# A deformable convolution after a recurrence: constants and borders placed before the recurrence, table rows written in 1 KB runs, the offsets' products ordered ahead of the turning

## The chip, the cores and the metric

The kernel runs on one core of one Trainium2 chip. The metric is the device time of one execution in microseconds, lower is better. Everything is float32, and one launch computes four layers of a network.

## The reference, cut to what matters

The input x has 4 images of 128 channels and 64 x 64 pixels. Each of four layers adds a convolution-like block and then a token block to x. The change lies where the token block of layer 0 (a recurrence) meets the convolution of layer 1 (a deformable one):

```
# layer 0, token block: tokens of an image in order, yt of 128 channels
Wx = batchnorm(layernorm(t) @ W.T)
yt = sigmoid(Wx[t] + yt @ V.T)            # one step after another
x  = x + y

# layer 1, deformable convolution, 3 x 3 taps
z    = layernorm over channels (x)
off  = conv3x3(z, w_off) + b_off          # 18 channels: dy, dx for each of 9 taps
mask = sigmoid(conv3x3(z, w_mod) + b_mod) # 9 channels
for each pixel and tap k:
    (py, px) = pixel + tap + (dy, dx)
    v = bilinear(z at the four pixels around (py, px), zero outside the image) * mask
x = x + sum over k of weight[:, :, k] @ v[k] + bias
```

## The kernel before, in words

x stays in SBUF as `net.xs`, channels on the 128 partitions, 4 x 4096 pixels along them. The phases follow one another in `PHASES`: `involution`, `recurrence`, `deformable`, then `expert_choice` and others. Inside a phase, `manual_schedule` fixes the order of PE, ACT, DVE and POOL to the order in which the Python code emits instructions; every engine works through its list in order. SP, which issues the ordinary transfers, also has one list in order. Transfers take turns over eight semaphores, so a transfer can wait for the one eight places before it. Where a pool's memory was used by an earlier phase, the first writer waits for that phase's last reader.

**Recurrence** (`recurrence`, lines 452 to 587). SP loads `rnn_w`, `rnn_wt`, `rnn_vt` and two vectors (L473 to L480). PE's first instruction is a product of `rnn_vt` with itself (L514); behind it come the layer norm (L181 and so on), the statistics, and two sweeps of the recurrence (L564, L569). The last sweep adds its states to `net.xs` (L575). POOL only clears two small tiles (L485).

**Deformable convolution** (`deformable`, lines 590 to 908). For each image a *table* in DRAM holds, for each of 66 x 66 positions, the 128 channels of the four pixels around it: 2 KB, so that one gathered row serves one bilinear sample. The code first loads the weights (`dcn_wk`, `dcn_woff`, `dcn_boff`, `dcn_bias`), clears `dcn_zero`, makes two grids of coordinates (L638, L640), and clears two padded images (`padded_pair`, L247). `plan(b)` then prepares one image:

- borders of the table are written from `dcn_zero` (L667, L669), 16 transfers per image;
- the layer norm into the padded image: centred products (L686), copies (L689), squares (L694), variances (L676), the root and reciprocal (L700, L704), and scaling (L710, L715);
- turning: for each of four groups of 16 rows, PE turns pixels onto 64 partitions (L724), ACT copies them to one of two `dcn_xt` buffers (L726), and SP writes that buffer four times to the table (L731), once for each of the four neighbours, 512 bytes per run;
- the offsets' products: 2 x 36 products over the padded image (L744), bias (L753), turning (L757), copies (L762);
- `places`: index and the four bilinear weights (L772 to L806), with the mask's sigmoid on ACT (L793).

For image 0 all of `plan(0)` comes first. Then, for each image, 288 gathers run on POOL (L816, 128 rows of 2 KB each), two to a step; ACT and DVE weight and add them (L830 to L841), PE turns and adds the two parts (L856, L857), ACT copies (L873), and PE multiplies by the tap's weight (L877). In every step one piece of `plan(b + 1)` is done beside it (`next(side, None)`), so images 1 to 3 are prepared during the gathers of the image before.

Of the kernel before, what the change touches and what calls it, by code (L numbers as in the profile page):

```python
# [17 lines left out]
F32 = mybir.dt.float32  # L18
BF16 = mybir.dt.bfloat16
I32 = mybir.dt.int32  # L20
# [4 lines left out]
PSUM = bass.MemoryType.PSUM  # L25
# [3 lines left out]
P = 128  # L29
B, H, W = 4, 64, 64  # L30
N = H * W
CH = 512
NCH = N // CH
ROWS = CH // W
NT = N // P
# [205 lines left out]
def padded_pair(net, pool, pad, name):  # L241

    side = H + 2 * pad
    out = []
    for i in range(2):
        t = pool.tile([P, side, side], F32, name=f"{name}{i}", bufs=1)
        net.nc.gpsimd.memset(t, 0.0)  # L247
        out.append(t)
    return out
# [202 lines left out]
def recurrence(net):  # L452
# [16 lines left out]
    with ExitStack() as ctx:  # L469
        sb = ctx.enter_context(tc.tile_pool(name="rnn", bufs=1))  # L470
        yp = ctx.enter_context(tc.tile_pool(name="rnn_y", bufs=3))
        w = sb.tile([P, P], F32, name="rnn_w")
# [31 lines left out]
        with (  # L504
# [34 lines left out]
            nc.vector.tensor_sub(shift, gb[:, 1:2], shift)  # L539

        ps = ctx.enter_context(tc.tile_pool(name="rnn_ps", bufs=2, space=PSUM))
        sums = net.xs.rearrange("p b (s t) -> p t b s", t=LEN)
# [46 lines left out]

def deformable(net):  # L590

# [3 lines left out]

    tc, nc, ins = net.tc, net.nc, net.ins
    KK, PAD = 9, 1  # L600
    SIDE = H + 2
    NO = 3 * KK
    Q4 = 4
    BANKS = {"pt": 3, "out": 2, "pd": 1, "pv": 1}
    GATHERED = 14
    with ExitStack() as ctx:
        dram = ctx.enter_context(tc.tile_pool(name="dcn_dram", bufs=1, space=bass.MemoryType.DRAM))
        tables = [dram.tile([SIDE, SIDE, 4, P], F32, name=f"dcn_table{b}") for b in range(B)]
        one = ctx.enter_context(tc.tile_pool(name="dcn", bufs=1))
        sb = ctx.enter_context(tc.tile_pool(name="dcn_s", bufs=2))  # L610
        ps = ctx.enter_context(tc.tile_pool(name="dcn_ps", bufs=2, space=PSUM))
# [4 lines left out]
        nc.sync.dma_start(woff[:, :, 2 * KK : NO], ins["L1_conv_w_mod"])  # L616
        boff = one.tile([P, 1], F32, name="dcn_boff")
        nc.vector.memset(boff, 0.0)
        for q in range(Q4):
            nc.sync.dma_start(boff[32 * q : 32 * q + 2 * KK], ins["L1_conv_b_off"])  # L620
            nc.sync.dma_start(boff[32 * q + 2 * KK : 32 * q + NO], ins["L1_conv_b_mod"])
        wk = one.tile([P, KK, P], F32, name="dcn_wk")
        nc.sync.dma_start(wk, ins["L1_conv_weight"])
        bias = one.tile([P, 1], F32, name="dcn_bias")
        nc.sync.dma_start(bias, ins["L1_conv_bias"])
        zero = one.tile([SIDE, P], F32, name="dcn_zero")
        nc.vector.memset(zero, 0.0)

        grids = []
        for axis in range(2):  # L630
            grid = one.tile([P, NT, KK], I32, name=f"dcn_grid{axis}")
            for half in range(2):
                p = slice(64 * half, 64 * half + 64)
                if axis == 0:
                    pattern, base, step = [[2, NT], [1, 3], [0, 3]], half - 1, 0
                else:
                    pattern, base, step = [[0, NT], [0, 3], [1, 3]], -1, 1
                nc.gpsimd.iota(grid[p], pattern=pattern, base=base, channel_multiplier=step)  # L638
            t = one.tile([P, NT, KK], F32, name=f"dcn_at{axis}")
            nc.vector.tensor_copy(t, grid)  # L640
            grids.append(t)
        pads = padded_pair(net, one, PAD, "dcn_pad")
# [7 lines left out]
        def plan(b):  # L650
# [6 lines left out]
            def bank(tag="pd" if b else "pt"):  # L657
                return ps.tile([P, CH], F32, name=f"dcn_{tag}", tag=tag, bufs=BANKS[tag])

            def inside(c):  # L660
                return xp[:, PAD + c * ROWS : PAD + (c + 1) * ROWS, PAD : PAD + W]


            for q in range(4):
                dy, dx = divmod(q, 2)
                for r in (H, H + 1) if dy else (0, H + 1):
                    nc.sync.dma_start(tables[b][r, :, q, :], zero)  # L667
                for x in (W, W + 1) if dx else (0, W + 1):
                    nc.sync.dma_start(tables[b][1 - dy : 1 - dy + H, x, q, :], zero[0:H])  # L669

# [35 lines left out]
            for c in range(NCH):  # L706
# [9 lines left out]
                yield  # L716
            for c2 in range(NCH // 2):

                xt = sb.tile([W, 2 * ROWS, P], F32, name="dcn_xt", tag="dcn_xt")
                for r0 in range(0, 2 * ROWS, 4):  # L720
                    pt = bank()[0:W].rearrange("p (r c) -> p r c", c=P)
                    for i in range(4):
                        r = PAD + c2 * 2 * ROWS + r0 + i
                        nc.tensor.transpose(pt[:, i, :], xp[:, r, PAD : PAD + W], net.ident)  # L724
                    yield
                    nc.scalar.copy(xt[:, r0 : r0 + 4, :], pt)  # L726
                    yield
                for q in range(4):
                    dy, dx = divmod(q, 2)
                    r0 = 2 * ROWS * c2 + 1 - dy  # L730
                    nc.sync.dma_start(  # L731
                        tables[b][r0 : r0 + 2 * ROWS, 1 - dx : 1 - dx + W, q, :].rearrange("r x c -> x r c"),
                        xt,
                    )

            off = sb.tile([P, NT, NO], F32, name="dcn_off", tag="dcn_off", bufs=1)
            for c4 in range(NCH // Q4):
# [25 lines left out]
                yield  # L763
            yield from places(b, off)

        def places(b, off):
# [32 lines left out]
            nc.vector.tensor_mul(lo, mask, ly)  # L799
            nc.vector.tensor_mul(wq[1], lo, lx)  # L800
            yield
# [3 lines left out]
            nc.vector.tensor_mul(wq[0], lo, lx)  # L805
            nc.vector.tensor_mul(wq[2], hi, lx)  # L806
            made[b] = (tables[b].rearrange("y x q c -> (y x) (q c)"), idx, wq)

        def taken(m, two):
# [876 lines left out]
def top2_experts(net):  # L1686
# [175 lines left out]
    involution,  # L1862
    recurrence,
    deformable,
    lambda net: expert_choice(net, 1),
# [83 lines left out]
```

## Time and profile before

The median of 3 runs is 8233.12 us (8232.96 to 8242.14). The profiled execution took 8237.43 us, of which 8235.6 are the span of its instructions. Busy time of the engines over that span and in three stretches of the stages concerned, in us:

| stretch (us from the span's start) | PE | DVE | ACT | POOL | clock of PE | DMA share |
|---|---|---|---|---|---|---|
| whole span, 8235.6 | 7626.6 | 5525.9 | 3801.2 | 5253.5 | 0.969 | |
| 1030.8 to 1236.7, recurrence | 183.5 | 104.8 | 77.0 | 0.0 | 0.95 | 0.00 |
| 1236.7 to 1331.7, head of the deformable convolution, before the first gather | 51.3 | 32.8 | 18.6 | 11.3 | 0.76 | 0.61 |
| 1331.7 to 2795.7, gathers | 1133.4 | 1247.6 | 638.0 | 1100.7 | 0.94 | 0.77 |

A row of a timeline gives: start in us, length in us, engine, line, operation, out<-in with the shape, and in brackets how long the engine sat idle before it and what released it. A matmul of float32 shows as two entries. PEld is the load of weights, SPq the issuing of transfers on SP. The DMA share is the mean occupied share of the core's 16 DMA engines. A wait for several things is put down to the one that the profile saw come last, which is not always the true one.

### The profile page before, as it was taken

Reading aid. Unit: us, or ns where it says so; the run is one execution under the profiler, and the core shown is the slowest. Engines: PE = TensorE matmul, PEld = TensorE weight load, DVE = VectorE, ACT = ScalarE, POOL = GpSimd, SP = SyncE. Lnnn points to the kernel's source line nnn. Section 1 sums busy time; section 2 is a strip of 40 time slices with the busy share of each in tenths; the row PEclk is TensorE's granted clock in tenths of the full one; section 3 lists DMA queues with packets and bytes.
Section 4 is the critical chain, followed back from the end, with each engine's and each line's share of the span. In section 5 each row is a group of like instructions: output and inputs, shape, how many; then the busy total and the mean of one; then the engine's idle time right before and its main releaser. Section 6 shows DMA issues by size and latency. Waiting matters only on the chain.

```text
span 8235.6 us, 146123 instructions
## 1 busy us (share of the span) xinstructions
PE 7626.6 (93%) x59726; PEld 3315.2 (40%) x59726; DVE 5525.9 (67%) x8715; ACT 3801.2 (46%) x7248; POOL 5253.5 (64%) x2925
## 2 busy tenths in 40 slices
PE   8999986777877889989999999999999999999899
PEld 2222243555555454443444344443444434444333
DVE  7888856888888632237767667766677667677155
ACT  4444433444444430323555555555555555555511
POOL 5989804777777400004888688887888878888700
PEclk9999998999999999988999999999999999999999
DMA  6434206877877430032554445544445445555400
GB/s 182 96 73 96 49 1 164 248 224 234 249 209 209 145 136 0 32 144 47 111 110 100 106 101 108 109 106 103 106 100 111 105 103 107 108 105 109 99 22 23
DMA packets 299127, 944.82 MB, mean 115 GB/s; under 512 B 41876, under 2 KB 114644, under 8 KB 240596
## 3 DMA queue, kind: packets, MB, share of 16 engines
q0 software_dynamic: 142848, 671.18, 34.6%
q1 hardware_dynamic: 155604, 264.26, 11.3%
q8 instruction: 469, 7.68, 0.4%
q14 instruction: 206, 1.69, 0.1%
HBM read 466.78 MB, written 65.88 MB: 65 GB/s over the span
## 4 chain that ended last, share of the span: by engine, by line
PE 57%; DVE 2%; issue 1%; DMA 1%; ACT 1%; POOL 0%; SPq 0%; DVEq 0%; ACTq 0%; POOLq 0%
PE att_pv L1552 15%; PE att_sc L1639 13%; PE att_mx L1496 11%; PE att_sc L1540 5%; PE conv_po L1306 3%; PE top_po L1852 3%; PE top_pw L1828 1%; DVE att_most L1507 1%; DMA moe_w<-in_L_ffn_weight 1%; PE att_sc L1469 0%; PE att_sc L1583 0%; PE top_po L1850 0%; PE att_sc L1600 0%; PE att_mx L1394 0%; PE att_sc L1430 0%
## 5 line engine op out<-in xcount | busy, mean ns | idle before, releaser
L1571 POOL TENSOR_TENSOR att_acc<-att_acc,att_ex 128x2048 f32<-128x2048 f32 x640 | 2902.0, 4534 | 638.5 <-ACT att_ex L1640 619.2
L1507 DVE TENSOR_REDUCE att_most<-att_mx 128x2 f32<-128x1024 f32 x2016 | 2461.8, 1222 | 1070.5 <-PE att_mx L1496 992.6
L1640 ACT ACTIVATE att_ex<-att_sc 128x512 f32<-128x512 f32 x4096 | 2222.9, 595 | 1771.4 <-PE att_sc L1639 1491.4
L1639 PE MATMUL att_sc<-att_q,att_k 32*128 32x512 f32 x8192 | 2455.7, 606 | 0.0
L1496 PE MATMUL att_mx<-att_k,att_q 32*128 32x512 f32 x8064 | 2292.2, 647 | 13.0 <-DVE att_parts L1519 10.8
L1540 PE MATMUL att_sc<-att_rows,att_ones_b 32*128 32x256 bf16 (+1 forms) x6144 | 1502.2, 306 | 4.7 <-ACT att_ex L1640 4.7
L816 POOL DMA_INDIRECT dcn_g<-dcn_table,dcn_idx x1152 | 1100.7, 955 | 436.9 <-DMA dcn_g<-dcn_table,dcn_idx 122.2
L1552 PE MATMUL att_pv<-att_ex,att_vals 128*32 128x256 f32 x16384 | 1309.8, 391 | 0.0
L1496 PEld LDWEIGHTS att_mx<-att_k,att_q 32*128 32x128 f32 x8064 | 610.9, 185 | 867.1 <-issue 707.6
L409 POOL TENSOR_TENSOR inv_prod<-inv_seen,inv_prod 128x512 f32<-128x512 f32 (+1 forms) x672 | 837.5, 1273 | 94.1 <-ACT inv_prod L408 94.1
L411 DVE SCALAR_TENSOR_TENSOR inv_prod<-inv_pk,bspan,inv_seen 128x512 f32<-128x512 f32 (+1 forms) x1120 | 774.6, 743 | 140.2 <-PE inv_pk L398 139.9
L1552 PEld LDWEIGHTS att_pv<-att_ex,att_vals 128*32 128x32 f32 x16384 | 322.5, 108 | 1318.9 <-issue 1300.8
L1639 PEld LDWEIGHTS att_sc<-att_q,att_k 32*128 32x128 f32 x8192 | 818.3, 183 | 10.7 <-issue 8.3
L830 ACT ACTIVATE dcn_one<-dcn_g,dcn_w 128x128 f32<-128x128 f32 x1152 | 457.5, 401 | 790.9 <-DMA dcn_g<-dcn_table,dcn_idx 787.6
L857 PE MATMUL dcn_pt<-ident,dcn_sum 128*128 128x128 f32 x2304 | 516.7, 308 | 242.6 <-DVE dcn_sum L841 241.8
L408 ACT ACTIVATE inv_prod<-inv_pk,bspan 128x512 f32<-128x512 f32 (+1 forms) x672 | 436.1, 682 | 503.8 <-PE inv_pk L398 503.8
L856 PE MATMUL dcn_pt<-ident,dcn_one 128*128 128x128 f32 x2304 | 482.9, 293 | 93.2 <-ACT dcn_st L873 81.1
L856 PEld LDWEIGHTS dcn_pt<-ident,dcn_one 128*128 128x128 f32 x2304 | 397.3, 203 | 305.7 <-issue 137.8
L398 PE MATMUL inv_pk<-inv_red,wtap 32*96 32x512 f32 (+1 forms) x3584 | 511.4, 636 | 7.4 <-DMA inv_seen<-inv_image 7.4
L857 PEld LDWEIGHTS dcn_pt<-ident,dcn_sum 128*128 128x128 f32 x2304 | 371.6, 203 | 322.1 <-DVE dcn_sum L841 321.0
L833 DVE TENSOR_SCALAR dcn_part<-dcn_g,dcn_w 128x128 f32<-128x128 f32 x1152 | 405.8, 352 | 122.5 <-DMA dcn_g<-dcn_table,dcn_idx 89.8
L420 PE MATMUL inv_out<-inv_prod,inv_fold 96*32 96x512 f32 (+1 forms) x3584 | 478.0, 605 | 8.5 <-DVE xs L428 8.5
(339 smaller groups left out, 7090.2 us busy)
## 6 DMA issues: line engine op xcount, KB each, us to landing
att_sum<-att_ex POOLq DMA_DIRECT2D x320, 1024.0 KB, 7.2
inv_seen<-inv_image SPq DMA_DIRECT2D x256, 266.0 KB
moe_w<-in_L_ffn_weight SPq DMA_DIRECT2D x64, 1024.0 KB
dcn_table<-dcn_xt SPq DMA_DIRECT2D x64, 512.0 KB
att_sum<-att_ex SPq DMA_DIRECT2D x32, 1024.0 KB
att_sum<-att_acc POOLq DMA_DIRECT2D x32, 1024.0 KB, 7.2
dcn_g<-dcn_table,dcn_idx POOLq DMA_INDIRECT x1152, 3.7
inv_image<-inv_rows SPq DMA_DIRECT2D x32, 304.0 KB
```

The lines of the kernel that those rows point to most:

```text
L409: nc.gpsimd.tensor_mul(of, view, of)
L411: nc.vector.scalar_tensor_tensor(out=of, in0=as_shape(pk[0:m], of), scalar=by, in1=view, op0=ALU.add, op1=ALU.mult)
L816: nc.gpsimd.indirect_dma_start(out=g, out_offset=None, in_=rows, in_offset=bass.IndirectOffsetOnAxis(ap=idx[:, j + i, k : k + 1], axis=0),)
L856: nc.tensor.matmul(out, one_, net.ident, start=i == 0, stop=False)
L857: nc.tensor.matmul(out, s, net.ident, start=False, stop=i == 3)
L1496: nc.tensor.matmul(pm[i] if alone else pm[:, i, :], q[r, t * P : (t + 1) * P], ks[r, kc * CH : (kc + 1) * CH], start=True, stop=True,)
L1507: nc.vector.tensor_reduce(most[:, 2 * half : 2 * half + 2, kc], pm, AX.X, ALU.max)
L1540: nc.tensor.matmul(pe[:, cols], ones_b[r], lows[g][r, cols], start=cols.start == 0, stop=False)
L1552: nc.tensor.matmul(block["pv"][r, cols], vals[b][:, t, r], ex[:, h, cols], start=t == 0 and half == 0, stop=t == NT - 1 and half == 1,)
L1571: nc.gpsimd.tensor_add(block["acc"], block["acc"], ex)
L1639: nc.tensor.matmul(pe, ks[r, t * P : (t + 1) * P], qs[c][r], start=False, stop=True)
L1640: nc.scalar.activation(ex[:, h, :], pe, AF.Exp)
```

## The change

`PHASES` now holds one phase `recurrence_and_deformable` in the place of two. It opens a pool `dcn_early`, makes a `Sampling` object in it, runs the recurrence, and then the deformable convolution.

- `Sampling` does, ahead of the recurrence in the code, what `deformable` did first: weights, `dcn_zero` (now 512 wide), the grids (one integer tile instead of two; clears and casts on POOL instead of DVE), and the borders of all four tables, now 24 transfers in all instead of 64.
- The table's four neighbours are ordered [dx][dy] instead of [dy][dx], so that two rows of the same column lie side by side. `dcn_xt` gets one more row, copied from the group before; each group is written by two transfers whose runs are two rows of 128 floats, 1 KB, taken from overlapping places of the buffer. After the last group the row below the image is written by two small transfers.
- In `plan` the turning stands behind the offsets' products instead of ahead of them.
- `padded_pair` clears only the four edges of each padded image.
- To make room: `dcn_one` has 14 buffers instead of 15, `dcn_sum` 13 instead of 15, and the pool `rnn_y` is opened only after the recurrence's first part. The weights `wq[1]` and `wq[2]` change places with the table's order.

```diff
@@ padded_pair
-        net.nc.gpsimd.memset(t, 0.0)
+        for edge in (t[:, 0:pad], t[:, pad + H :], t[:, :, 0:pad], t[:, :, pad + W :]):
+            net.nc.gpsimd.memset(edge, 0.0)
@@ recurrence
-        yp = ctx.enter_context(tc.tile_pool(name="rnn_y", bufs=3))
         w = sb.tile([P, P], F32, name="rnn_w")
...
+        yp = ctx.enter_context(tc.tile_pool(name="rnn_y", bufs=3))
         ps = ctx.enter_context(tc.tile_pool(name="rnn_ps", bufs=2, space=PSUM))
@@ 
+class Sampling:
+    def __init__(self, net, one, dram):
+        tc, nc, ins = net.tc, net.nc, net.ins
+        KK = 9
+        SIDE = H + 2
+        self.tables = [dram.tile([SIDE, SIDE, 2, 2, P], F32, name=f"dcn_table{b}") for b in range(B)]
+        zero = one.tile([SIDE, 4 * P], F32, name="dcn_zero")
+        nc.gpsimd.memset(zero, 0.0)
+
+        self.woff = woff = one.tile([P, KK, 32], F32, name="dcn_woff")
+        nc.gpsimd.memset(woff, 0.0)
+        nc.sync.dma_start(woff[:, :, 0 : 2 * KK], ins["L1_conv_w_off"])
+        nc.sync.dma_start(woff[:, :, 2 * KK : 3 * KK], ins["L1_conv_w_mod"])
+        self.boff = boff = one.tile([P, 1], F32, name="dcn_boff")
+        nc.gpsimd.memset(boff, 0.0)
+        for q in range(4):
+            nc.sync.dma_start(boff[32 * q : 32 * q + 2 * KK], ins["L1_conv_b_off"])
+            nc.sync.dma_start(boff[32 * q + 2 * KK : 32 * q + 3 * KK], ins["L1_conv_b_mod"])
+        self.wk = one.tile([P, KK, P], F32, name="dcn_wk")
+        nc.sync.dma_start(self.wk, ins["L1_conv_weight"])
+        self.bias = one.tile([P, 1], F32, name="dcn_bias")
+        nc.sync.dma_start(self.bias, ins["L1_conv_bias"])
+
+        self.grids = []
+        for axis in range(2):
+            grid = one.tile([P, NT, KK], I32, name="dcn_grid", tag="dcn_grid")
...
+                nc.gpsimd.iota(grid[p], pattern=pattern, base=base, channel_multiplier=step)
+            t = one.tile([P, NT, KK], F32, name=f"dcn_at{axis}")
+            nc.gpsimd.tensor_copy(t, grid)
+            self.grids.append(t)
+
+        for table in self.tables:
+            for y in (H, H + 1):
+                nc.sync.dma_start(table[y].rearrange("x a b c -> x (a b c)"), zero)
+            for dx in range(2):
+                for x in (W, W + 1) if dx else (0, W + 1):
+                    nc.sync.dma_start(table[0:H, x, dx].rearrange("y b c -> y (b c)"), zero[0:H, 0 : 2 * P])
+
+
+def recurrence_and_deformable(net):
+    with ExitStack() as ctx:
+        dram = ctx.enter_context(net.tc.tile_pool(name="dcn_dram", bufs=1, space=bass.MemoryType.DRAM))
+        one = ctx.enter_context(net.tc.tile_pool(name="dcn_early", bufs=1))
+        sampling = Sampling(net, one, dram)
+        recurrence(net)
+        deformable(net, sampling)
@@ deformable: its own constants, grids and borders are gone
-        woff = one.tile([P, KK, 32], F32, name="dcn_woff")
-        nc.vector.memset(woff, 0.0)
...
-            nc.vector.tensor_copy(t, grid)
-            grids.append(t)
...
-            for q in range(4):
-                dy, dx = divmod(q, 2)
-                for r in (H, H + 1) if dy else (0, H + 1):
-                    nc.sync.dma_start(tables[b][r, :, q, :], zero)
-                for x in (W, W + 1) if dx else (0, W + 1):
-                    nc.sync.dma_start(tables[b][1 - dy : 1 - dy + H, x, q, :], zero[0:H])
@@ plan: the turning, moved from ahead of the offsets' products to behind them
-            for c2 in range(NCH // 2):
-                xt = sb.tile([W, 2 * ROWS, P], F32, name="dcn_xt", tag="dcn_xt")
...
-                    nc.scalar.copy(xt[:, r0 : r0 + 4, :], pt)
-                    yield
-                for q in range(4):
-                    dy, dx = divmod(q, 2)
-                    r0 = 2 * ROWS * c2 + 1 - dy
-                    nc.sync.dma_start(
-                        tables[b][r0 : r0 + 2 * ROWS, 1 - dx : 1 - dx + W, q, :].rearrange("r x c -> x r c"),
-                        xt,
-                    )
...
+            before = None
+            for c2 in range(NCH // 2):
+                xt = sb.tile([W, 2 * ROWS + 1, P], F32, name="dcn_xt", tag="dcn_xt")
+                if before is None:
+                    nc.vector.memset(xt[:, 0, :], 0.0)
+                else:
+                    nc.scalar.copy(xt[:, 0, :], before[:, 2 * ROWS, :])
...
+                    nc.scalar.copy(xt[:, r0 + 1 : r0 + 5, :], pt)
+                    yield
+                pairs = bass.AP(
+                    tensor=xt.tensor, offset=xt.offset, ap=[list(xt.ap[0]), [P, 2 * ROWS], [1, 2 * P]]
+                )
+                r0 = 2 * ROWS * c2
+                for dx in range(2):
+                    nc.sync.dma_start(
+                        tables[b][r0 : r0 + 2 * ROWS, 1 - dx : 1 - dx + W, dx].rearrange("r x b c -> x r (b c)"),
+                        pairs,
+                    )
+                    if c2 == NCH // 2 - 1:
+                        nc.sync.dma_start(tables[b][H, 1 - dx : 1 - dx + W, dx, 0], xt[:, 2 * ROWS, :])
+                before = xt
             yield from places(b, off)
@@ taken
-                s = sb.tile([P, P], F32, name="dcn_one", tag="one", bufs=15)
+                s = sb.tile([P, P], F32, name="dcn_one", tag="one", bufs=14)
...
-                s = sb.tile([P, P], F32, name="dcn_sum", tag="sum", bufs=15)
+                s = sb.tile([P, P], F32, name="dcn_sum", tag="sum", bufs=13)
@@ PHASES
-    recurrence,
-    deformable,
+    recurrence_and_deformable,
```

More of the change, by code (lines that the diff above doesn't have):

```diff
@@ L587, in recurrence @@
             sweep(0, True, begin())
[L590 to L611, printed above, removed]
-        woff = one.tile([P, KK, 32], F32, name="dcn_woff")
-        nc.vector.memset(woff, 0.0)
+class Sampling:
[8 more added lines that the diff above has]
+        nc.gpsimd.memset(woff, 0.0)
@@ L615, in deformable @@
         nc.sync.dma_start(woff[:, :, 0 : 2 * KK], ins["L1_conv_w_off"])
[L616 to L619, printed above, removed]
+        nc.sync.dma_start(woff[:, :, 2 * KK : 3 * KK], ins["L1_conv_w_mod"])
+        self.boff = boff = one.tile([P, 1], F32, name="dcn_boff")
+        nc.gpsimd.memset(boff, 0.0)
+        for q in range(4):
             nc.sync.dma_start(boff[32 * q : 32 * q + 2 * KK], ins["L1_conv_b_off"])
-            nc.sync.dma_start(boff[32 * q + 2 * KK : 32 * q + NO], ins["L1_conv_b_mod"])
@@ L622, in deformable @@
[L622 to L629, printed above, removed]
+            nc.sync.dma_start(boff[32 * q + 2 * KK : 32 * q + 3 * KK], ins["L1_conv_b_mod"])
+        self.wk = one.tile([P, KK, P], F32, name="dcn_wk")
+        nc.sync.dma_start(self.wk, ins["L1_conv_weight"])
@@ L630, in deformable @@
+        self.bias = one.tile([P, 1], F32, name="dcn_bias")
+        nc.sync.dma_start(self.bias, ins["L1_conv_bias"])
+        self.grids = []
         for axis in range(2):
-            grid = one.tile([P, NT, KK], I32, name=f"dcn_grid{axis}")
+            grid = one.tile([P, NT, KK], I32, name="dcn_grid", tag="dcn_grid")
             for half in range(2):
@@ L639, in deformable @@
             t = one.tile([P, NT, KK], F32, name=f"dcn_at{axis}")
-            nc.vector.tensor_copy(t, grid)
-            grids.append(t)
+            nc.gpsimd.tensor_copy(t, grid)
[13 more added lines that the diff above has]
+        deformable(net, sampling)
+def deformable(net, sampling):
+    tc, nc = net.tc, net.nc
+    KK, PAD = 9, 1
+    SIDE = H + 2
+    NO = 3 * KK
+    Q4 = 4
+    BANKS = {"pt": 3, "out": 2, "pd": 1, "pv": 1}
+    GATHERED = 14
+    tables, woff, boff = sampling.tables, sampling.woff, sampling.boff
+    wk, bias, grids = sampling.wk, sampling.bias, sampling.grids
+    with ExitStack() as ctx:
+        one = ctx.enter_context(tc.tile_pool(name="dcn", bufs=1))
+        sb = ctx.enter_context(tc.tile_pool(name="dcn_s", bufs=2))
+        ps = ctx.enter_context(tc.tile_pool(name="dcn_ps", bufs=2, space=PSUM))
         pads = padded_pair(net, one, PAD, "dcn_pad")
@@ L716, in plan @@
                 yield
-            for c2 in range(NCH // 2):
-                xt = sb.tile([W, 2 * ROWS, P], F32, name="dcn_xt", tag="dcn_xt")
[L720 to L724, printed above, removed]
-                    yield
-                    nc.scalar.copy(xt[:, r0 : r0 + 4, :], pt)
-                    yield
-                for q in range(4):
-                    dy, dx = divmod(q, 2)
-                    r0 = 2 * ROWS * c2 + 1 - dy
-                    nc.sync.dma_start(
-                        tables[b][r0 : r0 + 2 * ROWS, 1 - dx : 1 - dx + W, q, :].rearrange("r x c -> x r c"),
-                        xt,
-                    )
             off = sb.tile([P, NT, NO], F32, name="dcn_off", tag="dcn_off", bufs=1)
@@ L763, in plan @@
                 yield
+            before = None
[5 more added lines that the diff above has]
+                    nc.scalar.copy(xt[:, 0, :], before[:, 2 * ROWS, :])
+                for r0 in range(0, 2 * ROWS, 4):
+                    pt = bank()[0:W].rearrange("p (r c) -> p r c", c=P)
+                    for i in range(4):
+                        r = PAD + c2 * 2 * ROWS + r0 + i
+                        nc.tensor.transpose(pt[:, i, :], xp[:, r, PAD : PAD + W], net.ident)
+                    yield
+                    nc.scalar.copy(xt[:, r0 + 1 : r0 + 5, :], pt)
+                    yield
+                pairs = bass.AP(
[10 more added lines that the diff above has]
+                before = xt
             yield from places(b, off)
@@ L799, in places @@
             nc.vector.tensor_mul(lo, mask, ly)
-            nc.vector.tensor_mul(wq[1], lo, lx)
+            nc.vector.tensor_mul(wq[2], lo, lx)
             yield
@@ L805, in places @@
             nc.vector.tensor_mul(wq[0], lo, lx)
-            nc.vector.tensor_mul(wq[2], hi, lx)
-            made[b] = (tables[b].rearrange("y x q c -> (y x) (q c)"), idx, wq)
+            nc.vector.tensor_mul(wq[1], hi, lx)
+            made[b] = (tables[b].rearrange("y x a b c -> (y x) (a b c)"), idx, wq)
         def taken(m, two):
```

## The prediction

> **What bounds the kernel now.** The page says which engine is busy over the whole span, but this change touches one seam: the end of the recurrence (1236.7 us into the span) and the head of the deformable convolution. The chain that ended last, asked for this stretch, gives no pieces, so I read the stage from the timelines of single engines. First POOL, because the convolution's long part (1331.7 to 2795 us) is its 1152 gathers:
>
> ```profile
> 1236.81 4.04 POOL L638 IOTA dcn_grid<- 64x288 int32 x4 [208.62 <-ACT rnn_y L569]
> 1240.91 7.39 POOL L247 MEMSET dcn_pad<- 128x4356 f32 x2
> 1331.70 1.22 POOL L816 DMA_INDIRECT dcn_g<-dcn_table,dcn_idx  x1 [83.39 <-DMA dcn_table<-dcn_zero]
> 1333.22 1.10 POOL L816 DMA_INDIRECT dcn_g<-dcn_table,dcn_idx  x1 [0.30 <-issue]
> 1334.63 0.95 POOL L816 DMA_INDIRECT dcn_g<-dcn_table,dcn_idx  x1 [0.30 <-issue]
> ```
>
> From the third gather on they come every 1.257 us (0.953 + 0.30); 1152 of them are 1448 us. All POOL idle before L816 is 436.9 us: 83.4 before the first, 1151 x 0.302 = 347.6 of issue, 5.9 of anything else. So after 1331.7 the stage is POOL's issue rate, and what the change can move is the time of the first gather. That gather needs the index and the whole table. What held each, on DVE, ACT and PE:
>
> ```profile
> 1240.89 7.58 DVE L640 CAST dcn_at<-dcn_grid 128x288 f32<-128x288 int32 x1 [0.88 <-POOL dcn_grid L638]
> 1248.39 1.87 DVE L689 COPY dcn_pad<-dcn_pt 128x512 f32<-128x512 f32 x3
> 1331.09 0.31 DVE L789 CAST dcn_idx<-dcn_row 128x288 int32<-128x288 f32 x1
> ...
> 1289.67 1.54 ACT L726 COPY dcn_xt<-dcn_pt 64x512 f32<-64x512 f32 x3 [11.45 <-DMA dcn_table<-dcn_xt]
> 1301.61 1.54 ACT L726 COPY dcn_xt<-dcn_pt 64x512 f32<-64x512 f32 x3 [9.63 <-DMA dcn_table<-dcn_xt]
> ...
> 1303.24 9.64 PE L744 MATMUL dcn_pv<-dcn_pad,dcn_woff 128*32 128x512 f32 x72
> ```
>
> DVE cannot start the norm before 1248.39, because POOL clears two whole padded images (7.39 us). The two turning buffers then wait for table writes, PE (in written order) stands behind them, the offsets' products start at 1303.24, and the index is ready at 1331.40: 0.30 before the first gather. The table lands near 1326 (the DMA share falls from 0.94 to 0.64 at 1324 and 0.38 at 1325), so the index comes last; the releaser named, a border write, is not it. The writes themselves, in 1290 to 1302 us:
>
> ```profile
> DMA packets 4226, 2.13 MB, mean 178 GB/s; under 512 B 64, under 2 KB 4226, under 8 KB 4226
> q1 hardware_dynamic: 4226, 2.13, 97.6%
> ```
>
> All 16 DMA engines are occupied at 178 GB/s. Last, the seam before, where the change puts work ahead of the recurrence's weights (SP, then PE):
>
> ```profile
> 1027.60 0.35 SPq L473 DMA_DIRECT2D rnn_w<-in_L_ffn_W  x1
> 1028.00 0.43 SPq L475 DMA_DIRECT2D rnn_wt<-in_L_ffn_Wt  x1
> 1028.47 0.43 SPq L477 DMA_DIRECT2D rnn_vt<-in_L_ffn_Vt  x1
> ...
> 1030.85 0.49 PE L514 MATMUL rnn_pb<-rnn_vt 128*128 128x128 f32 x2 [1.31 <-DVE xs L428]
> ```
>
> The involution's last reader of its buffers on POOL ends at 1027.6; only then do the weights start. PE's first product of the recurrence is L514, on rnn_vt, and it already runs as soon as the involution's last add (L428, ends 1030.79) is done. There is no slack for rnn_vt to come later.
>
> **What the Trainium skill says.** "SBUF — State Buffer", section "Door 1: The DMA port swizzle": partitions 0 to 63 reach 8 of 16 DMA ports, no more than 0 to 31, about 218 GB/s against 436. This trace agrees: the involution's loads into 32 partitions run at 202 GB/s (103 to 111 us, share full), its stores from 128 partitions at 386 (80 to 86 us); the table is written from 64. "DMA: Bandwidth & Descriptors", section "Why small descriptors are slow": some 3 cycles per packet beside its 32-byte beats. So 512 B costs 16 + 3 and 1 KB 32 + 3, per byte 8% less; no run shows 1 KB yet. That a port and not the packet is short fits one more row: beside gathers (1480 to 1520 us) a 512 B packet took 0.385 x 40 us x 16 / 7694 = 32 ns, alone (0.976 x 12 x 16 / 4226) 44 ns. "TensorE: Matmul & The Clock Gate", Part 1: after an idle window of about 3.4 us PE runs at half clock until it has been busy as long; here L686 takes 1.78 us at 1342.8 after a pause and 1.02 at 1323.6.
>
> **The change part by part.**
>
> 1. *Early constants.* The order of SP's instructions in the changed kernel, once built, has 36 transfers (wk, two of woff, eight of boff, bias, 24 borders) ahead of rnn_w, rnn_wt, rnn_vt. They wait for the same end of the involution (its buffers lie where the constants go), and woff also for POOL's clears of zero and woff. POOL clears 258 columns in 0.28 us and 4356 in 3.73, so 512 and 288 take 0.5 + 0.3: woff is issued at 1028.4. From there to the last small constant took 5.4 us before (1238.78 to 1244.20): 1033.8. Border writes before: two L667 0.92 us, two L669 1.09, 0.045 between pairs; 8 rows and 16 columns are 3.7 + 8.7 + 0.5 = 12.9 us: 1046.7. Descriptors per transfer stay 66 and 64, but bytes grow to 2.1 MB; at 178 GB/s that is 12 us, so issue and data are level (up to 2 us more if data is slower). rnn_w and rnn_wt 0.9: rnn_vt is issued at 1047.6 and lands about 2.0 later (before: at most 2.3), 1049.6. L514 slips from 1030.85 by **18.8 us** (17 to 22). All of the recurrence is behind it in PE's fixed order. PE has then idled 19 us: half clock for 3.4 us costs up to 1.7; I take 1.2. Together **+20.0**. The constants on POOL (four iotas 4.04 us, two casts) lie under the recurrence, where POOL is idle for 208.6 us; rnn_ends, cleared behind them at about 1034, is needed after 1168.
>
> 2. *Borders of the pads only.* Eight clears of 66 columns at about 0.15 us instead of 7.39, and no iota or DVE clears and casts after the recurrence: the first norm copy starts when DVE's last add ends (1238.45), not at 1248.39. PE then paces the copies as before: **-9.7 us** for the norm, which ends at 1262.8.
>
> 3. *Products before turning.* The offsets' block takes what it took (1303.24 to 1323.74: 20.5 us); PE's part starts at 1262.1 and ends at 1282.6 (up to 1.7 less if PE is warm). The index follows by 1290, no longer last. Turning starts at 1282.6; transposes and four copies took 4.3 us to the first write, about 3.1 with PE warm: the first table write is issued at 1285.7 instead of 1275.96, **+9.7 us**. The earlier norm is thus spent on the products, which used to lie beside the writes.
>
> 4. *1 KB runs.* The bytes are the same, 4 x 2 x 64 x 16 x 1 KB = 8.39 MB a table. At 178 GB/s 47.2 us; at 178 x (19/16)/(35/32) = 193 GB/s (estimate from the two pages) 43.5, plus 0.4 for the two single-row writes and the copied row. The two buffers still overlap: a pair takes 10.9 us, its refill about 3. Start 1.6 after issue (before: 87% share in the first 12 us), receipt and issue 0.6: 1285.7 + 1.6 + 43.9 + 0.6 = 1331.8; ACT's sigmoid, behind the last copies, and the weights are done by about 1318. First gather **+0.1**, say +0.5 for the extra copies on ACT. Bounds: no gain per byte, 178: +4; the full 218: -4.5; cost per packet only, 22.7 us of writing: -20.5.
>
> 5. *Buffers 15 to 14 and 13, rnn_y's pool placed later, extra copies and clears per batch:* nothing, since gathers pace POOL and PE follows the sums two steps behind (about 6 live); batches 1 to 3 now finish turning near step 94 of 144, some 125 us before they are needed. If that cover were gone, each late step would cost 2.5 us. The border transfers no longer lie behind the writes on SP; nothing waited for them.
>
> Sum: 20.0 + 0.5 = **+20.5 us**. The profiled execution took 8237.43 (span 8235.6 and 1.8 around it), so 8258; the median of runs is 4.3 lower, so 8233.1 + 20.5 = **8254 us**.
>
> **The rivals.** (a) *Writing is priced by the packet.* Halving the packets then halves the writing: first gather near 1312, and -20.5 pays for the late recurrence: 8234, no change. For it: the engines' share is 97.6%. Against: 32 ns in company and 202 GB/s at large packets into 32 partitions. It decides from about 215 GB/s on, where less than 0.2% is left. (b) *The weights are not late*, because SP takes the constants while the involution still runs: 8234. Against: woff and zero wait for POOL, whose last product is the involution's own. (c) *Borders limited by data and 1 KB without gain:* +22 + 1.7 + 4 = 8261. (d) Both (a) and (b), faster: 8214; nothing speaks for two at once.
>
> **How the numbers follow.** Mine 0.66 (8250 to 8259), (c) 0.06, (a) with rates between 215 GB/s and it 0.19, (b) 0.05, (d) 0.04. About 0.2% (16.5 us) is what a measurement can tell from no change. Slower: mine and (c), 0.72; same: (a), (b), 0.24; faster 0.04. The range 8237 to 8262 leaves out the lower part of (a) and (b), and (d).
>
> **What would show it.** Right: L514 starts near 1050 behind rnn_vt's transfer, with the 36 transfers ahead of it on SP; the first norm copy comes within 2 us of the recurrence's last add; the offsets' products end before the first table write; the first gather stands about 95 us after the recurrence's end as before, and is released by the table's write, with the index 40 us old; table writes run near 193 GB/s; the gather stage keeps 1464 us. Wrong: L514 near 1031, writes above 215 GB/s, or gathers off their 1.257 us.

## The result, and the profile after

The changed kernel takes 8257.39 us (median of 9 runs, 8253.91 to 8263.33); the kernel before, run beside it and before it, 8237.59 (9 runs, 8232.96 to 8245.8). The ratio is 1.0023, 95% interval 1.0015 to 1.0032: slower by some 20 us. The profiled execution of after took 8256.66 us, with a span of 8254.8, 19.2 more than before.

First the seam at the recurrence's start, from the timelines of SP and PE of the kernel after (columns as before: start, length, engine, line, operation, and in brackets the idle time ahead and its releaser):

```profile
1032.07 0.36 SPq L618 DMA_DIRECT2D dcn_bias<-in_L_conv_bias  x1
...
1043.50 2.37 SPq L639 DMA_DIRECT2D dcn_table<-dcn_zero  x4
1045.96 0.53 SPq L473 DMA_DIRECT2D rnn_w<-in_L_ffn_W  x1
1046.54 0.45 SPq L475 DMA_DIRECT2D rnn_wt<-in_L_ffn_Wt  x1
1047.04 0.42 SPq L477 DMA_DIRECT2D rnn_vt<-in_L_ffn_Vt  x1
...
1049.31 0.77 PE L514 MATMUL rnn_pb<-rnn_vt 128*128 128x128 f32 x2 [21.82 <-DMA rnn_wt<-in_L_ffn_Wt]
1049.88 6.56 PE L181 MATMUL rnn_pd<-xs,cent 128*128 128x512 f32 x12
```

`rnn_vt` is issued behind the last border write, and PE stands still for 21.82 us where it stood 1.31. The first twelve products then take 6.56 us instead of 5.62: PE is slow after its rest. Next, the head of the convolution, from the timelines of DVE, PE, SP and POOL of the kernel after:

```profile
1255.05 2.19 DVE L576 TENSOR_TENSOR xs<-xs,rnn_y 128x512 f32<-128x512 f32 x2 [0.32 <-ACT rnn_y L570]
1257.51 1.50 DVE L713 COPY dcn_pad<-dcn_pt 128x512 f32<-128x512 f32 x2 [0.27 <-issue]
...
1280.49 9.88 PE L750 MATMUL dcn_pv<-dcn_pad,dcn_woff 128*32 128x512 f32 x72
...
1303.99 27.09 SPq L792 DMA_DIRECT2D dcn_table<-dcn_xt  x7
...
1308.59 0.31 DVE L824 CAST dcn_idx<-dcn_row 128x288 int32<-128x288 f32 x1
...
1351.33 1.22 POOL L851 DMA_INDIRECT dcn_g<-dcn_table,dcn_idx  x1 [94.81 <-DMA dcn_table<-dcn_xt]
...
2801.79 0.95 POOL L851 DMA_INDIRECT dcn_g<-dcn_table,dcn_idx  x1 [0.30 <-DMA dcn_g<-dcn_table,dcn_idx]
```

The same landmarks in the kernel before, from its timelines of PE, DVE, SP and POOL:

```profile
1031.17 5.62 PE L181 MATMUL rnn_pd<-xs,cent 128*128 128x512 f32 x12
...
1236.27 2.18 DVE L575 TENSOR_TENSOR xs<-xs,rnn_y 128x512 f32<-128x512 f32 x2 [0.29 <-ACT rnn_y L569]
...
1275.96 42.35 SPq L731 DMA_DIRECT2D dcn_table<-dcn_xt  x16
...
2784.96 0.95 POOL L816 DMA_INDIRECT dcn_g<-dcn_table,dcn_idx  x1 [0.30 <-DMA dcn_g<-dcn_table,dcn_idx]
```

The norm now starts 0.27 us behind the recurrence's last add (9.94 before). The products come first, the index is ready at 1308.9, and the first gather, released by the table, comes 42 us after that. And the writing, in the view of the transfers for 1310 to 1325 us of the kernel after:

```profile
DMA packets 2835, 2.85 MB, mean 190 GB/s; under 512 B 48, under 2 KB 2835, under 8 KB 2835
...
q1 hardware_dynamic: 2835, 2.85, 96.3%
```

Runs of 1 KB move at 190 GB/s; runs of 512 bytes moved at 178.

The difference at the first gather (1331.70 to 1351.33) is made of four pieces: the recurrence's last add ends 18.79 us later; from it to the norm's first copy takes 9.67 less; from there to the first table write 18.91 more (46.48 against 27.57); from there to the first gather 8.40 less (47.34 against 55.74). The sum is 19.63. The gathers themselves take 1450.5 us instead of 1453.3, and the rest of the kernel 5453.0 instead of 5450.6.

### The profile page after: what moved, and what is told of

It is laid out like the page before. It is cut to its first block, busy times and chain, and to the rows that moved or that the text cites. A ratio compares the mean times of both kernels' runs of the same rounds, so it can differ in the third digit from the quotient of the medians.

```text
span 8254.8 us, 146108 instructions
## 1 busy us (share of the span) xinstructions
PE 7612.6 (92%) x59726; PEld 3313.3 (40%) x59726; DVE 5517.4 (67%) x8714; ACT 3803.0 (46%) x7260; POOL 5232.3 (63%) x2942
## 4 chain that ended last, share of the span: by engine, by line
PE 57%; DVE 2%; issue 1%; DMA 1%; ACT 1%; POOL 0%; SPq 0%; DVEq 0%; ACTq 0%; POOLq 0%
PE att_pv L1587 15%; PE att_sc L1674 13%; PE att_mx L1531 11%; PE att_sc L1575 5%; PE conv_po L1341 3%; PE top_po L1887 3%; PE top_pw L1863 1%; DVE att_most L1542 1%; DMA moe_w<-in_L_ffn_weight 1%; PE att_sc L1504 0%; PE att_sc L1635 0%; PE att_sc L1618 0%; PE top_po L1885 0%; PE att_sc L1465 0%; PE att_mx L1429 0%
```

## The experiments

A run-to-run spread of some 6 us either way hides parts of the size in question, so each kernel is read at its landmarks first (profiled executions, us) and by its median second.

| kernel | L514, first matmul of the recurrence | last add to norm's first copy | norm's first copy to first gather | first gather | first to last gather |
|---|---|---|---|---|---|
| before | 1030.85 | 9.94 | 83.31 | 1331.70 | 1453.3 |
| after | 1049.31 | 0.27 | 93.82 | 1351.33 | 1450.5 |
| weights first | 1033.14 | 0.31 | 93.89 | 1334.90 | 1449.0 |
| weights and turning first | 1034.51 | 0.32 | 81.95 | 1322.36 | 1451.3 |
| after, runs of 512 | 1049.38 | 0.29 | 96.65 | 1352.23 | 1449.1 |
| before, edges only | 1031.11 | 3.46 | 82.56 | 1326.01 | 1457.9 |
| 128 partitions, turning first | 1029.75 | 0.27 | 56.29 | 1293.82 | 1442.5 |
| 128 partitions, products first | 1032.94 | 0.28 | 80.23 | 1322.58 | 1440.8 |
| 128 partitions, products between | 1031.40 | 0.27 | 58.77 | 1297.77 | 1443.7 |

**1. The weights first (step 1).** From after: the tiles are still allocated ahead, but their clears and transfers are issued behind the recurrence's loads.

```diff
 def recurrence_and_deformable(net):
-        recurrence(net)
+        recurrence(net, sampling)
 def recurrence(net, sampling):
         nc.sync.dma_start(gb[:, 1:2], ins["L0_ffn_beta"])
+        sampling.fill(net)
```

> The kernel after, with one thing moved: the constants' and borders' 36 transfers and clears are issued behind the recurrence's own loads of w, wt, vt and gamma/beta instead of in front of them; everything else is as in the changed kernel. My theory (step 1: the recurrence is late because its three weights stand behind 36 issues of about 0.55 us on SP's in-order queue): the recurrence's first matmul starts about 2.8 us after the involution's last square instead of 21.8, the recurrence's end, the first gather and the kernel's end all come 18 to 20 us earlier than after, the kernel takes about 8238.5 us (8236 to 8242), that is, level with before (0.999 to 1.001), and the 36 transfers vanish beside the 206 us recurrence. Rival (the recurrence is late because its matrices' memory is taken over from the involution's buffers, or because the border data fill the DMA engines): the first matmul stays near 1049 and the time near 8257.

Measured: 8242.95 us, ratio to before 1.0005 (0.9997 to 1.0013). From the timelines of SP, PE and POOL of this kernel:

```profile
1030.89 0.43 SPq L477 DMA_DIRECT2D rnn_vt<-in_L_ffn_Vt  x1
...
1033.14 0.77 PE L515 MATMUL rnn_pb<-rnn_vt 128*128 128x128 f32 x2 [5.06 <-DMA dcn_boff<-in_L_conv_b_mod]
...
1334.90 1.22 POOL L854 DMA_INDIRECT dcn_g<-dcn_table,dcn_idx  x1 [94.87 <-DMA dcn_table<-dcn_xt]
```

`rnn_vt` is issued 16 us earlier, L514 starts 16.2 earlier and the first gather 16.4. Nothing but the order on SP and POOL differs, so the place in the order is shown to be the cause, and the memory taken over from the involution is not. The other half of the rival, that the borders' data fill the DMA engines, is not separated by this run, since the data move with the issues. The timelines speak against it: in after, L514 starts 2.3 us after the issue of `rnn_vt` (at most 2.4 in before), the DMA share from 1034 to 1048 us is 0.57, and a pair of row borders takes 0.93 us to issue with 132 KB each, where it takes 0.92 in before with 33 KB. So the weights waited for the issuing and not for the bytes. The gain is 2 to 4 us less than I expected: four constants still stood ahead of the weights, as SP's timeline has it, and the first products were slow here too (6.51 us). The 32 transfers that now stand behind the weights cost nothing that shows.

**2. The turning first again (step 3).** From the kernel of experiment 1, the block that turns and writes goes back ahead of the products; 1 KB runs and edge clears stay.

```diff
+            before = None
+            for c2 in range(NCH // 2):
...
             off = sb.tile([P, NT, NO], F32, name="dcn_off", tag="dcn_off", bufs=1)
...
-            before = None
-            for c2 in range(NCH // 2):
...
             yield from places(b, off)
```

> The kernel with the weights first as in the run before, and besides the turning and writing of the table put back ahead of the offsets' products; runs of 1 KB and edge-only clears stay. My theory (step 3: products ahead of the turning hold back the first table write by about 19 us while the index is ready long before it is wanted): the first table write is issued about 19 us earlier than in the kernel with the weights first, the index becomes the later of the two or level with the table (both about 1318 to 1321 counted as in the kernel before), the first gather comes 11 to 13 us earlier, and the kernel takes 8225 to 8229 us, a ratio to before of 0.9984 to 0.9990. Rival (the products cost nothing where they stand, since the table's writing is what takes the time): no change against the kernel with the weights first, 8237 to 8240.

Measured: 8229.97 us, ratio to before 0.9991 (0.9983 to 1.0000); the first gather is 12.5 us earlier than in experiment 1. From the timelines of ACT, DVE and POOL of this kernel:

```profile
1280.60 0.30 ACT L752 COPY dcn_xt<-dcn_xt 64x128 f32<-64x128 f32 x1 [10.73 <-DMA dcn_table<-dcn_xt]
...
1303.62 0.69 ACT L791 ACTIVATE dcn_om<-dcn_pv,dcn_boff 128x512 f32<-128x512 f32 x1 [9.46 <-PE dcn_pv L782]
...
1321.75 0.31 DVE L827 CAST dcn_idx<-dcn_row 128x288 int32<-128x288 f32 x1
...
1322.36 1.22 POOL L854 DMA_INDIRECT dcn_g<-dcn_table,dcn_idx  x1 [83.01 <-DVE dcn_idx L827]
```

Which of the two comes last depends on the order: products first, the table ends the wait; turning first, the index does, 0.3 us before the gather. Turning first costs less, since the products and the writes then run side by side. The price is the stall seen at 1280.60: ACT and PE stand behind two turning buffers that wait for their writes.

**3. Runs of 512 bytes in after (step 4).** Same layout and order, four transfers per group instead of two.

```diff
-                    nc.sync.dma_start(
-                        tables[b][r0 : r0 + 2 * ROWS, 1 - dx : 1 - dx + W, dx].rearrange("r x b c -> x r (b c)"),
-                        pairs,
-                    )
...
+                    for dy in range(2):
+                        r0 = 2 * ROWS * c2 + 1 - dy
+                        nc.sync.dma_start(
+                            tables[b][r0 : r0 + 2 * ROWS, 1 - dx : 1 - dx + W, dx, dy].rearrange("r x c -> x r c"),
+                            xt[:, 1 : 2 * ROWS + 1, :],
+                        )
...
```

(Two transfers of a single row stand ahead of the first group here, instead of behind the last one.)

> The kernel after, with its table written in four transfers of 512-byte runs per group instead of two of 1 KB; layout, order and all else as after. My theory (step 4: the writes are bound by the ports behind 64 partitions, not by a price per packet): bytes move at 178 instead of 190 GB/s, the last write lands 3 to 4 us later, the kernel takes 8260 to 8262 us. Rival a (a price per packet, so that halving the number of packets nearly halved the time): the last write lands about 20 us later and the kernel takes about 8277.

Measured: 8254.92 us, ratio to before 1.0021 (1.0012 to 1.0030), which cannot be told from after. From the timelines of SP and POOL, and the view of the transfers for 1310 to 1325 us, of this kernel:

```profile
1301.88 42.16 SPq L790 DMA_DIRECT2D dcn_table<-dcn_xt  x16
...
1352.23 1.22 POOL L849 DMA_INDIRECT dcn_g<-dcn_table,dcn_idx  x1 [97.67 <-DMA dcn_table<-dcn_xt]
```

```profile
DMA packets 5287, 2.67 MB, mean 178 GB/s; under 512 B 80, under 2 KB 5287, under 8 KB 5287
```

From the first group's write to the first gather are 50.35 us, against 47.34 in after: 3.0 us, and 178 against 190 GB/s. The packet-priced rival, at 20 us, falls. The median points 2.5 us the other way, within the spread; only the trace shows these 3 us.

**4. Edges only, in before (step 2).**

```diff
-        net.nc.gpsimd.memset(t, 0.0)
+        for edge in (t[:, 0:pad], t[:, pad + H :], t[:, :, 0:pad], t[:, :, pad + W :]):
+            net.nc.gpsimd.memset(edge, 0.0)
```

> The kernel before, with one thing changed: the padded images are cleared along their edges only. My theory (step 2): the clears on GpSimd shrink from 9.7 us to about 3, GpSimd still makes the grids ahead of them (about 4 us), so the first copy of the norm starts about 6 us earlier (near 1242 instead of 1248.4), the first gather as well, and the kernel takes 8229 to 8233 us, a ratio of 0.9990 to 0.9995. Rival (the norm is held by VectorE's own work behind the recurrence and not by the clears): the first copy moves by under 1 us and the time stays at 8237.

Measured: 8232.55 us, ratio to before 0.9992 (0.9986 to 0.9999). From the timelines of DVE and POOL of this kernel:

```profile
1242.41 1.12 DVE L641 CAST dcn_at<-dcn_grid 128x288 f32<-128x288 int32 x1 [0.88 <-POOL dcn_grid L639]
1243.45 2.58 DVE L690 COPY dcn_pad<-dcn_pt 128x512 f32<-128x512 f32 x4
...
1326.01 1.22 POOL L817 DMA_INDIRECT dcn_g<-dcn_table,dcn_idx  x1 [82.65 <-DMA dcn_table<-dcn_zero]
```

The copy comes 3.46 us after the last add instead of 9.94: 6.5 us from the clears alone. DVE's cast, which waits for the grid, now holds it; after has no such cast there, which is the other 3.2. The cast itself is worth a look: a cast of the same shape and types takes 0.31 us elsewhere (L777 of before), but this one lasts 1.12 us here and 7.58 in before (L640), in both until 0.2 us after POOL's clears end (1243.37 and 1248.30). So DVE was held up beside the clears; whether the norm's copy would also have waited for them by itself is not shown. The first gather gains 5.7 us and the median 5.1; in the profiled execution the gathers gave most of that back (1457.9 us), which the median does not bear out.

**5. The table from 128 partitions (step 4's cause).** From the kernel of experiment 2. The padded image is turned 128 consecutive positions at a time, its borders included, so that a group of eight blocks lies on all 128 partitions; four writes per group in runs of 512 bytes; four turning buffers; and the recurrence's weights in a pool of their own.

```diff
-        w = sb.tile([P, P], F32, name="rnn_w")
+        w, wt, vt = weights
...
+        first = ctx.enter_context(net.tc.tile_pool(name="rnn_first", bufs=1))
+        weights = [first.tile([P, P], F32, name=f"rnn_{n}") for n in ("w", "wt", "vt")]
...
+            for g0 in range(0, FLAT // P, 8):
+                n = min(8, FLAT // P - g0)
+                xt = sb.tile([P, 8, P], F32, name="dcn_xt", tag="dcn_xt", bufs=4)
...
+                        nc.tensor.transpose(pt[:, i, :], flat[:, r : r + P], net.ident)
...
+                for dx in range(2):
+                    for dy in range(2):
+                        at = g0 * P + SIDE + 1 - SIDE * dy - dx
+                        nc.sync.dma_start(
+                            tables[b][at : at + n * P, 2 * dx + dy].rearrange("(g p) c -> p g c", p=P), xt[:, 0:n, :]
+                        )
```

> The kernel with weights first and the turning ahead of the products, and the table written in another way: the padded image is turned 128 consecutive positions at a time (35 transposes of 128x128 instead of 64 of 128x64), so each group leaves from 128 partitions in four transfers of 512-byte runs, borders included (9.17 MB per image instead of 8.39), no border transfers but two per table; the recurrence's weights have memory of their own, so that their loads wait for nothing. My theory (step 4: ports behind 64 partitions set the 178 to 190 GB/s): the same 512-byte runs from 128 partitions move at 300 GB/s or more, the first image's last write lands 27 to 32 us after its first is issued, and the first gather waits for the index alone; it comes 75 to 77 us after the norm's first copy instead of 82, and the kernel takes 8219 to 8225 us. Rival (44 ns per 512-byte packet whatever the partition, that is 17,920 packets over 16 engines): still about 180 GB/s, the last write lands about 50 us after the first is issued; the first gather hardly differs, so the rate decides and not the time.

Measured: 8189.05 us, ratio to before 0.9945 (0.9932 to 0.9959): 47 us faster than before. From the view of the transfers for 1265 to 1285 us, and the timelines of SP, ACT, DVE and POOL, of this kernel:

```profile
DMA packets 13705, 6.93 MB, mean 346 GB/s; under 512 B 208, under 2 KB 13704, under 8 KB 13704
```

```profile
1263.16 25.47 SPq L765 DMA_DIRECT2D dcn_table<-dcn_xt  x20
...
1270.97 0.48 ACT L760 COPY dcn_xt<-dcn_pt 128x384 f32<-128x384 f32 x1 [4.02 <-DMA dcn_table<-dcn_xt]
...
1292.63 0.31 DVE L822 CAST dcn_idx<-dcn_row 128x288 int32<-128x288 f32 x1
...
1293.82 1.42 POOL L849 DMA_INDIRECT dcn_g<-dcn_table,dcn_idx  x1 [57.08 <-DVE dcn_frac L830]
```

Packets of the same 512 bytes move at 346 GB/s, 1.94 times the 178 of experiment 3. So it is not the packet that limited the writes. The Trainium skill, "SBUF — State Buffer", section "Door 1: The DMA port swizzle", gives twice as many ports to 128 partitions as to 64, which fits the factor. The grouping of the rows and the table's layout changed together with the partitions, so the ports as the cause are supported and not shown alone. The expected time was missed by 30 us on the good side. I had the index ready 75 us after the norm's first copy, worked out from the kernel before; it was ready after 55. And the gathers took 11 us less than before. The next runs go after both.

**6. Products first, and products between.** The same kernel with the turning behind the products, or with three groups ahead of them and two behind.

```diff
-            for g0 in range(0, FLAT // P, 8):
+            for g0 in range(0, 24, 8):
...
             yield from places(b, off)
+            for g0 in range(24, FLAT // P, 8):
```

(Shown for the second; its two groups stand ahead of `places`.)

> As the kernel that writes from 128 partitions, with the offsets' products ahead of the turning as in the changed kernel. The index is then ready about 51 us after the norm's first copy and the first write is issued about 47 us after it. My theory (ports): table landed 30 us after that, first gather 78 to 80 us after the norm's first copy, kernel 8221 to 8228. Rival (price per packet): first gather 97 to 99 us after the norm's first copy, kernel 8240 to 8246.

> As the kernel that writes from 128 partitions, with three of the five groups turned ahead of the offsets' products and two behind them. My theory (ports): index about 56 us and last write about 66 us after the norm's first copy, first gather 66 to 70 us after it (82 in the kernel with the turning first, 83.3 before), kernel 8209 to 8217 us, faster than before by 0.25 to 0.35%. Rival (price per packet): last write lands about 78 us after the norm's first copy, kernel 8222 to 8230.

Measured: products first 8213.31 us, ratio 0.9974 (0.9964 to 0.9985); between 8191.07, ratio 0.9945 (0.9932 to 0.9959). Both are below the expected times. From the timelines of SP and POOL of the kernel with the products first:

```profile
1287.69 31.47 SPq L793 DMA_DIRECT2D dcn_table<-dcn_xt  x20
...
1322.58 1.22 POOL L848 DMA_INDIRECT dcn_g<-dcn_table,dcn_idx  x1 [81.02 <-issue]
```

And of the kernel with the products between:

```profile
1287.00 6.90 SPq L812 DMA_DIRECT2D dcn_table<-dcn_xt  x8
...
1297.77 1.22 POOL L867 DMA_INDIRECT dcn_g<-dcn_table,dcn_idx  x1 [59.54 <-issue]
```

The first gather comes 80.2 us after the norm's first copy, where the changed kernel, with the same order and 64 partitions, needs 93.8. From the first write to the first gather it takes 34.9 us instead of 47.3, which is most of the 13.6; four buffers are in that too. Between gains nothing over turning first (58.8 against 56.3), against my expectation: turning first, index (1292.9) and table (last packets near 1291.8) now end together, 1 to 2 us ahead of the gather; between, the index is as early (1293.1), but the two groups turned last come later (last packets near 1296.6) and the gather waits for them until 1297.77.

**7. Two turning buffers instead of four.**

```diff
-                xt = sb.tile([P, 8, P], F32, name="dcn_xt", tag="dcn_xt", bufs=4)
+                xt = sb.tile([P, 8, P], F32, name="dcn_xt", tag="dcn_xt", bufs=2)
```

> As the kernel that writes from 128 partitions with the turning ahead of the products, but with two turning buffers instead of four. It tells apart why that kernel's index was ready 55 us after the norm's first copy and not 75 as expected, and why its gathers took 1442 us and not 1450. Theory: ACT's copies no longer stand waiting for a buffer while the products' biases and the batches' sums queue behind them. With two buffers they wait again (8 transposes' worth of data takes 6 us to write plus about 3 until it is seen), the first gather comes 63 to 66 us after the norm's first copy instead of 56, and the gathers take 1446 us or more; the kernel takes 8197 to 8205 us. Rival (the rate alone does it; two buffers are enough once writing is fast): first gather 56 to 58 us after the first copy, gathers 1441 to 1444, kernel 8187 to 8193.

> The kernel with two turning buffers once more, beside the one with four on the same chip: the chip of the run before granted a lower clock (0.934), so its gathers, 1525 us, cannot be set against the 1442 of the kernel with four. Left to tell: with two buffers the first gather comes 67 us after the norm's first copy (56 with four), and, if waits for turning buffers are also what stretched the gathers of before and after, the gathers take 4 us or more longer than with four buffers; if not, they agree within 2 us.

> The kernel with four turning buffers again: first gather 56 us after the norm's first copy, 0.9945 of before.

These three were run on two other chips, where all kernels take some 4% longer (the kernel before 8562.82 and 8591.39 us). There PE's clock is 0.78 to 0.80 during the gathers instead of 0.94. With the same code, four buffers, the gathers take 1791.1 us there and 1442.5 in experiment 5, which is nearly all of the 362 us between the two spans. So only ratios and the head, where the clock hardly differs, can be compared across chips. Two buffers: 8541.0 us, 0.9973 (0.9961 to 0.9984), and again 8560.12, 0.9966 (0.9954 to 0.9979). Four, beside the second: 8552.39, 0.9957 (0.9940 to 0.9974). From the timelines of ACT and POOL of the first of them:

```profile
1277.89 1.07 ACT L760 COPY dcn_xt<-dcn_pt 128x512 f32<-128x512 f32 x2 [4.84 <-DMA dcn_table<-dcn_xt]
1284.07 0.48 ACT L760 COPY dcn_xt<-dcn_pt 128x384 f32<-128x384 f32 x1 [5.11 <-DMA dcn_table<-dcn_xt]
1284.44 0.69 ACT L786 ACTIVATE dcn_om<-dcn_pv,dcn_boff 128x512 f32<-128x512 f32 x1
...
1305.46 1.42 POOL L849 DMA_INDIRECT dcn_g<-dcn_table,dcn_idx  x1 [67.74 <-DVE dcn_frac L830]
```

The products' bias (L786) stands behind the last copy in ACT's list and comes at 1284.44; with four buffers it came at 1274.50. The first gather comes 67.0 and 66.9 us after the norm's first copy, and 56.2 with four buffers. So of the 25.7 us between 81.95 (experiment 2) and 56.29 (experiment 5), the buffers make 10.7. The writes are as fast with two buffers as with four, 345 GB/s from 1265 to 1285 us, so more buffers are not what raised the rate in experiment 5. The other 15 us belong to the faster writes and the 35 instead of 64 transposes, which these runs do not separate.

Did waiting for buffers also lengthen the gathers? From the timeline of POOL, first and last gather with two buffers (the second of these runs):

```profile
1305.36 1.42 POOL L849 DMA_INDIRECT dcn_g<-dcn_table,dcn_idx  x1 [67.71 <-DVE dcn_frac L830]
...
3094.87 0.94 POOL L849 DMA_INDIRECT dcn_g<-dcn_table,dcn_idx  x1 [0.30 <-issue]
```

And with four, on the same chip:

```profile
1295.85 1.42 POOL L849 DMA_INDIRECT dcn_g<-dcn_table,dcn_idx  x1 [57.04 <-DVE dcn_frac L830]
...
3086.98 0.94 POOL L849 DMA_INDIRECT dcn_g<-dcn_table,dcn_idx  x1 [0.30 <-issue]
```

The gathers take 1789.5 us with two buffers and 1791.1 with four, so here they are not lengthened. Of the first gather's lead of 9.5 us, 7.9 are left at the last one, and the medians differ by 7.7. On the faster chips, where the gathers follow one another with less waiting, this was not tried, so what shortened them in experiment 5 stays open.

## Why the prediction was right

It said +20.5 us and 8254; the runs gave +19.8 and 8257.4. The difference of level is the median of the kernel before: 8233.12 in the three runs that I had, 8237.59 in nine. The correction by 4.3 us from the profiled execution to the median was taken from too few runs. That the size agrees within 0.7 us is in part luck. In the profiled executions the recurrence ended 1.2 us less late than said, and the gathers, said to keep their pace, took 2.8 us less; the rest of the kernel took 2.4 more and the writing 1.2 more, neither of which was forecast. These nearly cancel.

1. *Early constants, +20.0.* The mechanism is shown by experiment 1. L514 came at 1049.31 (said: 1049.6). The last add moved by 18.8; L514 alone by 18.5, and the slow first products cost 1.2 as taken, so the recurrence itself took about 0.9 less, which is within what it varies: from L514 to the last add's end it took 205.6 to 209.1 us in these profiles. That the weights would not be late (rival b) fell. I had called the borders' issue and data level; with a DMA share of 0.57 over the borders the issuing alone set the pace, and rival (c) with its slow borders fell.
2. *Edges only, -9.7.* Measured -9.67. Experiment 4 splits it: 6.5 from the clears, the rest from the iotas and casts moved away.
3. *Products before turning, +9.7 with the earlier norm in it.* From the norm's first copy to the first write 18.9 more, said: 19.4; the index came 51.4 us after that copy, said: 51.5. Experiment 2 shows that the step costs 12.5 us at the first gather (11.9 counted from the norm's first copy). Without it, and with the weights first, the kernel is at 0.9991 of before, with an interval that just reaches 1: what is left of the change is at best a small gain.
4. *1 KB runs.* 190 GB/s where I had estimated 193 from the Trainium skill (step 4 of the prediction), and 47.34 us from first write to first gather where I had 46.1. The 1.2 us are the sum of three differences: the data began to move 1.2 us after the first issue (said: 1.6), moved for 44.9 us (said: 43.9), and the gather came 1.2 us after the last packet, at 1350.1 (said: 0.6, for receipt and issue). For transfers that GpSimd issues, the Trainium skill, "DMA: Bandwidth & Descriptors", section "Anatomy of one DMA", says that most of a fixed 2 us is the write's receipt, with HBM as the heaviest target. These writes were issued by SP, and no run splits their 1.2 us into receipt and issue. Rival (a), a price per packet, had 0.19 and is settled by experiments 3 and 5: halving the packets gained 7%, and packets of 512 bytes ran at nearly twice the rate from 128 partitions.
5. *Buffers and gathers, nothing.* The gathers took 2.8 us less, where I had said that they would keep their pace. This is a balance. POOL is busy with them for 9.4 us less (947 ns each instead of 955), and idle between them for 6.6 us more. The added idle time lies in ten gaps of 0.7 to 2.1 us, where before had three of 0.9 to 1.4; they fall while the next image's table is written or just behind it. What shortened the single gathers and what opened the gaps was not tested.

What the prediction did not see is that its own reading, 64 partitions behind half of the ports, pointed to a change worth more than all of this one.

## What to carry to other kernels

A queue that issues in order carries whatever stands first in the code: 32 small transfers, at 0.3 to 0.6 us each to issue, cost 16 us ahead of three weights that the next stage needs at once, and nothing that shows behind them. When transfers are slow with all DMA engines occupied, ask which partitions they leave from before making their runs longer: 1 KB runs gained 7% in rate, writing from 128 partitions instead of 64 gained 94% (59% in one kernel). And where an engine copies into buffers that wait for transfers, look at what is queued behind those copies: two more buffers were worth 11 us at the first gather, though no transfer became faster.

## What the runs showed of the hardware that I had not expected

- Writes from 128 partitions to the table ran at 346 GB/s in packets of 512 bytes, but at 283 in the kernel with the products first (1290 to 1310 us), with the same transfers. No run explains the difference.
- Gathers in the two kernels whose border transfers lie between the tables' writes took 955 and 957 ns each, in the seven others at the higher clock 947 to 949. This goes together with the borders; that they cause it was not shown.
- On the two chips where PE's clock is 0.78 to 0.80 during the gathers, the stage takes 1775 to 1791 us, against 1441 to 1458 us on the others, though a single gather takes as long (948 to 949 ns). No run shows that the clock alone causes this. The version with 128 partitions is at 0.9957 of before there and at 0.9945 on the faster chip, with intervals that overlap.
